# A recommender on one core: wide row buffers, scores summed in one PSUM bank, and an item stage with its products in PSUM

## The chip, the core and the metric

The kernel runs on one core of a Trainium2 chip. Its time is device microseconds from start to end of one launch. A core has five engines with their own instruction queues: TensorE (PE; its weight loads are listed apart as PEld), VectorE (DVE), ScalarE (ACT), GpSimd (POOL) and SyncE (SP). They meet through semaphores. SBUF is the working memory with 128 partitions; PSUM is the memory that TensorE writes, in banks of 512 float32 values per partition, eight of them. All data here is float32.

## The reference

Two stages follow each other. The first makes, for each of 50,001 items, two attention vectors over its 32 neighbours. The second scores 100 history positions of each of 16,384 users against the user's target item.

```python
def _neighbor_attn(E, near_full):                 # E_in or E_out, 50001 x 32
    V = E[near_full]                              # 50001 x 32 neighbours x 32
    scores = einsum('nd,nkd->nk', E, V) / sqrt(32)
    w = softmax(scores, axis=-1)
    return einsum('nk,nkd->nd', w, V)
a_sus = _neighbor_attn(E_in, near_full)
a_inf = _neighbor_attn(E_out, near_full)
h = concat([E_hist[history], a_sus[history], a_inf[history]])    # users x 100 x 128
t = concat([E_tgt[target], a_inf[target], a_sus[target]])        # users x 128
x = h * t[:, None, :]
z = relu(einsum('bld,hd->blh', x, W1) + b1)       # 128 hidden
scores = einsum('blh,h->bl', z, W2[0])
exp_A = exp(scores) * ((history != target[:, None]) & (history != 0))
denom = sum(exp_A, axis=-1) ** 0.5
s = sum(h * (exp_A / denom[:, None])[..., None])  # one number for all users
pred = dot(s, t) / (|s| * |t|)                    # s broadcast to 128 values
return sigmoid(pred)
```

Because only the sum over everything is needed of `h * attn`, a position enters `s` as its weight times the sum of its row's 128 values.

## The kernel before

**Item stage** (lines 106 to 257). Items are taken 128 at a time, one item to a partition: a *sub*, 391 of them, in 23 loads of 17 subs. For each sub POOL issues 32 indirect DMAs (`gather`, L136), one per neighbour; each fetches 128 rows of 64 values, that neighbour's E_in and E_out for each of the 128 items, into a buffer `v` (a ring of five subs). On DVE follow `products` (L152: `v` times the items' own rows, which ACT has copied into PSUM at L146; 2,048 values per partition, written to `prod` in SBUF), `scores` (L162: sums over 32), `largest` (L170, L171), on ACT `exponents` (L179, with the sums), then on DVE `weighted` (L192, once for each table: `v` times the exponents, written to `wv` in SBUF in the order d, k), `attend` (L203 a reciprocal, L205 sums over the neighbours) and `attended` (L212). `prod` and `wv` have one buffer each, in the pool `n_p`. In each turn of the loop POOL gets the gathers of sub s, DVE first the weighted rows of sub s-2, then the products and scores of sub s-1; a row is finished three subs late. After 17 subs the finished rows go to a table in DRAM: 129 values per item, first the sum of the other 128.

**User stage** (lines 268 to 408). Users are taken 128 at a time (a *chunk*, 128 of them) and positions 4 at a time (a *group*, 25 in a chunk), 3,200 groups in all. For each group s:

- `gather(s)`: POOL issues 4 indirect DMAs (L325), each fetching one position's row of 129 values for the 128 users, into a row buffer `h`. The ring has HBUF = 20 such buffers, one group each.
- `turn(s)`: PE turns the 4 row blocks by transposes into PSUM, `hT_ps` (L341, 3 banks).
- `times_target(s)`: DVE multiplies by the turned target row (L346, 128x512, PSUM to SBUF), and copies the 4 row sums of the group to `hsum` (L349, 128x4). That copy is the last reader of the row buffer. A declaration (L353, L354) tells the planner that the copy needs no wait of its own on the gathers, since PE has already read the rows.
- `hidden(s-3)`: PE multiplies W1 by the 512 columns into `z_ps` (L358, 3 banks), and ACT adds the bias and takes the relu (L360).
- `scored(s-6)`: PE makes the 4 positions' scores (L367): each of the four blocks of z, 128x128, is the stationary operand, and W2, one column, is the moving one, so that a score column of 128 users results. The chunk's 100 columns lie in one bank, `score`.

Every float32 product on PE shows as two passes, each with its own weight load, where it is a matmul, and as one where it is a transpose. Once per chunk POOL fetches the next chunk's target rows (`target_rows`, L289, at group 5), PE, DVE and ACT prepare them (`target_work`, L301 to L315, at group 15), and, after a chunk's last score, ACT takes the exponents of the 100 scores (`weights`, L373) and two groups later DVE masks, weighs with `hsum` and sums (`ended`, L378 to L381).

The order of the work is written out by hand for PE, ACT, DVE, SP and, in the user stage, POOL: each engine runs its instructions in the order of the calls in the loop at L388. POOL's queue holds only the gathers and the target rows there; it may run ahead of PE until the ring of row buffers is full. A short last stage (lines 410 to 440) makes `s` and the predictions.

Of the kernel before, what the change touches and what calls it, by code (L numbers as in the profile page):

```python
# [10 lines left out]
F32 = mybir.dt.float32  # L11
# [3 lines left out]
AF = mybir.ActivationFunctionType  # L15
# [3 lines left out]
P = 128  # L19
ITEMS = 50001  # L20
K = 32
G = 32
DE = 64
D = 128
HID = 128
B = 16384
L = 100
# [14 lines left out]
UC = B // P  # L42
BSUB = 4
LG = 4
NG = L // LG
W = 1 + D
LAG = 3
HBUF = 20

# [1 line left out]
def kernel(  # L53
# [52 lines left out]
    with (  # L106
        tc.manual_schedule(engines={E.Activation, E.DVE, E.SP}),
        tc.tile_pool(name="n_in", bufs=2) as n_in,
        tc.tile_pool(name="n_v", bufs=5) as n_v,
        tc.tile_pool(name="n_p", bufs=1) as n_p,  # L110
        tc.tile_pool(name="n_s", bufs=3) as n_s,
        tc.tile_pool(name="n_ps", bufs=2, space=bass.MemoryType.PSUM) as n_ps,
    ):
        its = {}
        subs = {}
# [32 lines left out]

        def products(s):
            v = subs[s]["v"]  # L150
            prod = n_p.tile([P, K, 2, G], F32, name="prod")
            nc.vector.tensor_tensor(  # L152
                prod.rearrange("p k t d -> p k (t d)"),
                v.rearrange("p k t d -> p k (t d)"),
                subs[s]["own"].to_broadcast([P, K, 2 * G]),
                ALU.mult,
            )
            subs[s]["prod"] = prod
# [29 lines left out]

        def weighted(s, t):
            if t == 0:  # L190
                subs[s]["wv"] = n_p.tile([P, 2, G, K], F32, name="wv")
            nc.vector.tensor_tensor(  # L192
                subs[s]["wv"][:, t].rearrange("p d k -> p k d"),
                subs[s]["v"][:, :, t, :],
                subs[s]["ex"][0][:, t, :]
                .rearrange("p (k o) -> p k o", o=1)
                .to_broadcast([P, K, G]),
                ALU.mult,
            )
# [67 lines left out]
    nc.vector.tensor_copy(tidf, tidx)  # L267
    with (
        tc.manual_schedule(engines={E.PE, E.Activation, E.DVE, E.SP, E.Pool}),
        tc.tile_pool(name="u_in", bufs=4) as u_in,  # L270
        tc.tile_pool(name="u_t", bufs=3) as u_t,
        tc.tile_pool(name="u_h", bufs=HBUF) as u_h,
        tc.tile_pool(name="u_x", bufs=6) as u_x,
        tc.tile_pool(name="u_z", bufs=6) as u_z,
        tc.tile_pool(name="u_s", bufs=3) as u_s,
        tc.tile_pool(name="ps_t", bufs=3, space=bass.MemoryType.PSUM) as ps_t,
        tc.tile_pool(name="ps_z", bufs=3, space=bass.MemoryType.PSUM) as ps_z,
        tc.tile_pool(name="ps_s", bufs=2, space=bass.MemoryType.PSUM) as ps_s,
    ):
        users, hists = {}, {}  # L280
        rows, got, hT, xT, z = {}, {}, {}, {}, {}

        def history_of(i):
            hists[i] = u_in.tile([P, BSUB, L], I32, name="hidx")
            nc.sync.dma_start(hists[i], hist_v[i])

        def target_rows(c):
            t = u_t.tile([P, D], F32, name="t")
            nc.gpsimd.indirect_dma_start(  # L289
                out=t,  # L290
                out_offset=None,
                in_=ttab[0:ITEMS, :],
                in_offset=bass.IndirectOffsetOnAxis(ap=tidx[:, c : c + 1], axis=0),
            )
            users[c] = {"t": t, "hidx": hists[c // BSUB][:, c % BSUB, :]}

        def target_work(c):
            u = users[c]
            t = u["t"]
            tT_ps = ps_t.tile([P, LG, P], F32, name="hT_ps")  # L300
            nc.tensor.transpose(tT_ps[:, 0, :], t, ident)  # L301
            tT = u_t.tile([D, 1, P], F32, name="tT")
            nc.vector.tensor_copy(tT[:, 0, :], tT_ps[:, 0, :])  # L303
            u["tT"] = tT
            nc.vector.tensor_reduce(tsum[:, c : c + 1], t, AX.X, ALU.add)
            junk = u_t.tile([P, D], F32, name="junk")
            nc.scalar.activation(junk, t, AF.Square, accum_out=tsq[:, c : c + 1])
            keep = u_s.tile([P, L], F32, name="keep")
            idf = u_s.tile([P, L], F32, name="idf")
            nc.vector.tensor_copy(idf, u["hidx"])  # L310
            nc.vector.tensor_scalar(keep, idf, 0.0, None, ALU.not_equal)  # L311
            nc.vector.scalar_tensor_tensor(
                keep, idf, tidf[:, c : c + 1], keep, ALU.not_equal, ALU.mult
            )
            u["keep"] = keep  # L315
            u["hsum"] = u_s.tile([P, L], F32, name="hsum")

        def gather(s):
            c, g = divmod(s, NG)
            rows[s] = u_h.tile([P, LG, W], F32, name="h")  # L320
            got[s] = []
            for q in range(LG):
                l = g * LG + q
                got[s].append(
                    nc.gpsimd.indirect_dma_start(  # L325
                        out=rows[s][:, q, :],
                        out_offset=None,
                        in_=table,
                        in_offset=bass.IndirectOffsetOnAxis(
                            ap=users[c]["hidx"][:, l : l + 1], axis=0  # L330
                        ),
                    )
                )

        def turn(s):
            c, g = divmod(s, NG)
            if g == 0:
                users[c]["score"] = ps_s.tile([P, L], F32, name="score")
            hT[s] = ps_t.tile([P, LG, P], F32, name="hT_ps")
            for q in range(LG):  # L340
                nc.tensor.transpose(hT[s][:, q, :], rows[s][:, q, 1:W], ident)  # L341

        def times_target(s):
            c, g = divmod(s, NG)
            xT[s] = u_x.tile([D, LG, P], F32, name="xT")
            nc.vector.tensor_tensor(  # L346
                xT[s], hT.pop(s), users[c]["tT"].to_broadcast([D, LG, P]), ALU.mult
            )
            copy = nc.vector.tensor_copy(  # L349
                users[c]["hsum"][:, g * LG : (g + 1) * LG],  # L350
                rows.pop(s)[:, :, 0:1].rearrange("p q o -> p (q o)"),
            )
            for one in got.pop(s):  # L353
                tc.declare_no_dep(copy.ins, one.ins, reason="TensorE has read the row")  # L354

        def hidden(s):
            z_ps = ps_z.tile([HID, LG, P], F32, name="z_ps")
            nc.tensor.matmul(z_ps, w1T, xT.pop(s), start=True, stop=True)  # L358
            z[s] = u_z.tile([HID, LG, P], F32, name="z")
            nc.scalar.activation(z[s], z_ps, AF.Relu, bias=b1_sb)  # L360

        def scored(s):
            c, g = divmod(s, NG)
            of = z.pop(s)
            for q in range(LG):
                l = g * LG + q
                nc.tensor.matmul(  # L367
                    users[c]["score"][:, l : l + 1], of[:, q, :], w2_sb, start=True, stop=True
                )

        def weights(c):
            users[c]["ea"] = u_s.tile([P, L], F32, name="ea")
            nc.scalar.activation(users[c]["ea"], users[c]["score"], AF.Exp)  # L373

        def ended(c):
            u = users.pop(c)
            ea = u["ea"]
            nc.vector.tensor_tensor(ea, ea, u["keep"], ALU.mult)  # L378
            nc.vector.tensor_reduce(den[:, c : c + 1], ea, AX.X, ALU.add)
            nc.vector.tensor_tensor(ea, ea, u["hsum"], ALU.mult)  # L380
            nc.vector.tensor_reduce(num[:, c : c + 1], ea, AX.X, ALU.add)  # L381

        last = UC * NG
        history_of(0)
        history_of(1)
        target_rows(0)
        target_work(0)
        for s in range(last + 2 * LAG + 4):  # L388
            c, g = divmod(s, NG)
            if s < last:  # L390
                if g == 0 and c % BSUB == 2 and 0 < c // BSUB and c // BSUB + 1 < UC // BSUB:
                    history_of(c // BSUB + 1)
                if g == 5 and c + 1 < UC:
                    target_rows(c + 1)
                gather(s)
                turn(s)
                times_target(s)
            if 0 <= s - LAG < last:
                hidden(s - LAG)
            if 0 <= s - 2 * LAG < last:  # L400
                scored(s - 2 * LAG)
            if s < last and g == 15 and c + 1 < UC:
                target_work(c + 1)
            done, left = divmod(s - 2 * LAG - NG, NG)
            if 0 <= done < UC and left == 0:
                weights(done)
            if 0 <= done < UC and left == 2:
                ended(done)

    with (  # L410
# [85 lines left out]
```

## Time and profile before

| | before |
| --- | --- |
| median of 3 runs | 36,684.49 us (36,681.49 to 36,691.43) |
| the profiled execution | 36,756.47 us, span 36,754.7 us |
| POOL, busy | 25,507.5 us, 69% |
| PE, PEld, busy | 10,981.4 us, 8,186.8 us |
| DVE, ACT, busy | 7,047.7 us, 2,610.8 us |
| item stage's gathers (L136) | 12,512, of 1,063 ns |
| user stage's gathers (L325) | 12,800, of 944 ns |
| mean granted clock of TensorE | 0.806 |

The profile is of one execution, which took 0.2% more than the median. Busy time is the time that an engine spends in its instructions. A gather on POOL is the issuing of the DMA, not the transfer, and the time between two instructions of an engine is its idle time, for which the profile names the event that ended it: `<-PE hT_ps L341` is a release by that PE instruction, `<-issue` means that nothing the profile shows was waited for, `<-remote` an event that it couldn't place. The granted clock is the share of full speed at which TensorE was let run: 1.00 in the item stage, where it does nothing, 0.63 on average in the user stage. In a timeline the columns are the start in us, the duration in us (the whole of a run of several equal instructions, x4 or so), the engine, the line, the operation, output and input, and in brackets the idle time ahead and what ended it.

### The profile page before, as it was taken

The numbers are of one execution on the slowest core, as the hardware profiler recorded it, in microseconds if no ns is written. First come the engines' busy times: TensorE is split into PE (matmuls) and PEld (weight loads), VectorE is DVE, ScalarE is ACT, GpSimd is POOL, SyncE is SP. The second block draws the span as 40 slices with busy tenths as digits, with TensorE's granted clock in tenths as the row PEclk, the third lists the DMA queues.
The fourth block names the chain that finished last, engine by engine and source line by source line (L and its number), as shares of the span: only waits on it lengthen the run. The fifth ranks groups of instructions, "written<-read, shape, count | busy, mean of one in ns | idle before, by whom it ended". The sixth has DMA issues, their size and how long they took to land. (4 is left out here: it accounts for less than half of the span.)

```text
span 36754.7 us, 143134 instructions
## 1 busy us (share of the span) xinstructions
PE 10981.4 (30%) x44931; PEld 8186.8 (22%) x44931; DVE 7047.7 (19%) x11109; ACT 2610.8 (7%) x5939; POOL 25507.5 (69%) x25446
## 2 busy tenths in 40 slices
PE   0000000000000000000455555555655555555555
PEld 0000000000000000000344444444444444444444
DVE  2222222222222222222111111111111111111111
ACT  0000000000000000000011111111111111111111
POOL 7777777777777777777666666666666666666665
PEclk9999999999999999999766666666666666666666
DMA  2111111111111111111222222222222222222221
GB/s 45 27 27 27 28 29 27 27 27 28 29 27 27 27 28 29 27 27 25 46 45 46 45 45 45 45 45 45 46 45 45 45 45 45 45 45 46 45 45 42
DMA packets 1028113, 1364.80 MB, mean 37 GB/s; under 512 B 559904, under 2 KB 614432, under 8 KB 1027360
## 3 DMA queue, kind: packets, MB, share of 16 engines
q0 software_dynamic: 814080, 1265.42, 16.4%
q10 hardware_dynamic: 151056, 51.51, 0.8%
q1 hardware_dynamic: 62224, 38.72, 0.4%
q8 instruction: 363, 5.95, 0.1%
q14 instruction: 390, 3.19, 0.0%
HBM read 1315.31 MB, written 51.50 MB: 37 GB/s over the span
## 5 line engine op out<-in xcount | busy, mean ns | idle before, releaser
L325 POOL DMA_INDIRECT h<-table,hidx x12800 | 12082.2, 944 | 6909.5 <-issue 3729.2
L136 POOL DMA_INDIRECT v<-in_egeo_dram,nidx x12512 | 13303.8, 1063 | 4199.3 <-issue 4100.5
L367 PEld LDWEIGHTS score<-w_sb,z 128*128 128x128 f32 x25600 | 5121.1, 264 | 7324.3 <-issue 7320.0
L367 PE MATMUL score<-w_sb,z 128*128 128x1 f32 x25600 | 4332.3, 273 | 5204.9 <-issue 5113.3
L301 PE MATMUL hT_ps<-ident,t 128*128 128x128 f32 x128 | 51.7, 404 | 17563.1 <-DMA t<-ttab,tidx 17527.7
L346 DVE TENSOR_TENSOR xT<-hT_ps,tT 128x512 f32<-128x512 f32 x3200 | 2190.4, 688 | 16114.5 <-PE hT_ps L341 7697.5
L358 PE MATMUL z_ps<-xT,w1T 128*128 128x512 f32 x6400 | 5005.9, 868 | 591.3 <-issue 588.1
L301 PEld LDWEIGHTS hT_ps<-ident,t 128*128 128x128 f32 x128 | 37.5, 293 | 17567.4 <-issue 17567.4
L341 PE MATMUL hT_ps<-ident,h 128*128 128x128 f32 x12800 | 3058.8, 360 | 2398.3 <-issue 1944.6
L360 ACT ACTIVATE z<-z_ps,b_sb 128x512 f32<-128x512 f32 x3200 | 2141.1, 687 | 17012.9 <-remote 6338.4
L152 DVE TENSOR_TENSOR prod<-v,own_ps 128x2048 f32<-128x2048 f32 x391 | 894.1, 2287 | 12667.3 <-DMA v<-in_egeo_dram,nidx 12667.1
L341 PEld LDWEIGHTS hT_ps<-ident,h 128*128 128x128 f32 x12800 | 2227.0, 205 | 2779.0 <-issue 2252.2
L358 PEld LDWEIGHTS z_ps<-xT,w1T 128*128 128x128 f32 x6400 | 1439.6, 270 | 881.5 <-issue 880.6
L192 DVE TENSOR_TENSOR wv<-v,ex 128x1024 f32<-128x1024 f32 x782 | 1407.6, 1876 | 341.9 <-ACT ex L179 240.0
L179 ACT ACTIVATE ex<-sc,top 128x32 f32<-128x32 f32 x782 | 227.7, 291 | 16996.0 <-DVE top L170 11999.4
L162 DVE TENSOR_REDUCE sc<-prod 128x64 f32<-128x2048 f32 x391 | 894.5, 2288 | 13.6
L205 DVE TENSOR_REDUCE att<-wv 128x64 f32<-128x2048 f32 x391 | 893.7, 2286 | 12.7
L349 DVE COPY hsum<-h 128x4 f32<-128x4 f32 x3200 | 544.0, 170 | 0.0
L289 POOL DMA_INDIRECT t<-ttab,tidx x128 | 120.8, 944 | 66.1 <-issue 65.2
L179 ACT ACTIVATION_READ_ACCUMULATOR ex<-sc,top 128x1 f32 x782 | 145.7, 186 | 0.0
L303 DVE COPY tT<-hT_ps 128x128 f32<-128x128 f32 x128 | 37.0, 289 | 423.8 <-remote 180.7
L212 DVE TENSOR_TENSOR row<-att,tot 128x64 f32<-128x64 f32 x391 | 88.1, 225 | 13.6
(50 smaller groups left out, 809.0 us busy)
## 6 DMA issues: line engine op xcount, KB each, us to landing
h<-table,hidx POOLq DMA_INDIRECT x12800
v<-in_egeo_dram,nidx POOLq DMA_INDIRECT x12512
table<-row ACTq DMA_DIRECT2D x22, 1096.5 KB
own<-in_egeo_dram SPq DMA_DIRECT2D x23, 544.0 KB
row<-in_ehist_dram SPq DMA_DIRECT2D x23, 544.0 KB
ttab<-in_etgt_dram ACTq DMA_DIRECT2D x1, 12500.0 KB
ttab<-row ACTq DMA_DIRECT2D x22, 544.0 KB
hidx<-in_history_dram SPq DMA_DIRECT2D x32, 200.0 KB
```

The lines of the kernel that those rows point to most:

```text
L136: nc.gpsimd.indirect_dma_start(out=v[:, k].rearrange("p t d -> p (t d)"), out_offset=None, in_=egeo, in_offset=bass.IndirectOffsetOnAxis(a ...
L152: nc.vector.tensor_tensor(prod.rearrange("p k t d -> p k (t d)"), v.rearrange("p k t d -> p k (t d)"), subs[s]["own"].to_broadcast([P, K, ...
L162: nc.vector.tensor_reduce(sc.rearrange("p t k -> p k t"), subs[s]["prod"], AX.X, ALU.add)
L192: nc.vector.tensor_tensor(subs[s]["wv"][:, t].rearrange("p d k -> p k d"), subs[s]["v"][:, :, t, :], subs[s]["ex"][0][:, t, :] .rearrange( ...
L205: nc.vector.tensor_reduce(att, subs[s]["wv"], AX.X, ALU.add)
L325: nc.gpsimd.indirect_dma_start(out=rows[s][:, q, :], out_offset=None, in_=table, in_offset=bass.IndirectOffsetOnAxis(ap=users[c]["hidx"][: ...
L341: nc.tensor.transpose(hT[s][:, q, :], rows[s][:, q, 1:W], ident)
L346: nc.vector.tensor_tensor(xT[s], hT.pop(s), users[c]["tT"].to_broadcast([D, LG, P]), ALU.mult)
L349: copy = nc.vector.tensor_copy(users[c]["hsum"][:, g * LG : (g + 1) * LG], rows.pop(s)[:, :, 0:1].rearrange("p q o -> p (q o)"),)
L358: nc.tensor.matmul(z_ps, w1T, xT.pop(s), start=True, stop=True)
L360: nc.scalar.activation(z[s], z_ps, AF.Relu, bias=b1_sb)
L367: nc.tensor.matmul(users[c]["score"][:, l : l + 1], of[:, q, :], w2_sb, start=True, stop=True)
```

## The change

- Row buffers. A buffer `h` now holds HG = 5 groups, 20 positions, and the ring has HBUF = 5 of them. Gathers write slices of it; PE and DVE read slices of it. The row sums are copied once for five groups (128x20), after the fifth of them has been multiplied; that copy is the last reader of the buffer. The declaration now names the 20 gathers.
- Scores. W2 is now the stationary operand: a group's weights are a window of 25 columns on a padded row `w2_row`, with W2 in column g and zeros elsewhere, and the group's z, 512 columns, is the moving operand. The 25 groups' products are accumulated in one PSUM bank, `turned` (25x512): row g gets group g's scores, the other rows get zeros added. When the chunk is done ACT copies the bank to SBUF (`kept`, one 25x512 copy), two groups later PE turns it back by four transposes (`turned_back`) into `score` (128 users x 4 x 25), and the exponents and the closing sums follow four and six groups after the last score, where they followed at zero and two. The loop runs four turns longer.
- PSUM. The hidden products have two banks instead of three; `score` has one bank of its own, `turned` two.
- Item stage. The pool `n_p` is gone: `prod` and `wv` share one PSUM tile, `big`, of four banks, with one buffer.

```diff
-HBUF = 20
+HG = 5
+HBUF = 5
...
-        tc.tile_pool(name="n_p", bufs=1) as n_p,
+        tc.tile_pool(name="n_pb", bufs=1, space=bass.MemoryType.PSUM) as n_pb,
...
-            prod = n_p.tile([P, K, 2, G], F32, name="prod")
+            prod = n_pb.tile([P, K * 2 * G], F32, name="big")
+            prod = prod.rearrange("p (k t d) -> p k t d", k=K, t=2)
...
-                subs[s]["wv"] = n_p.tile([P, 2, G, K], F32, name="wv")
+                wv = n_pb.tile([P, K * 2 * G], F32, name="big")
+                subs[s]["wv"] = wv.rearrange("p (t d k) -> p t d k", t=2, k=K)
...
-        tc.tile_pool(name="ps_z", bufs=3, space=bass.MemoryType.PSUM) as ps_z,
+        tc.tile_pool(name="ps_z", bufs=2, space=bass.MemoryType.PSUM) as ps_z,
...
+        tc.tile_pool(name="ps_1", bufs=1, space=bass.MemoryType.PSUM) as ps_1,
...
+        w2_row = u_1.tile([HID, 2 * NG - 1], F32, name="w2_row")
+        nc.vector.memset(w2_row, 0.0)
+        nc.vector.tensor_copy(w2_row[:, NG - 1 : NG], w2_sb)
...
-            rows[s] = u_h.tile([P, LG, W], F32, name="h")
-            got[s] = []
+            k = g % HG
+            if k == 0:
+                wide[s] = u_h.tile([P, HG * LG, W], F32, name="h")
+                got[s] = []
+            rows[s] = wide[s - k][:, k * LG : (k + 1) * LG, :]
...
+            rows.pop(s)
+            if g % HG < HG - 1:
+                return
+            s0, l = s - HG + 1, (g - HG + 1) * LG
             copy = nc.vector.tensor_copy(
-                users[c]["hsum"][:, g * LG : (g + 1) * LG],
-                rows.pop(s)[:, :, 0:1].rearrange("p q o -> p (q o)"),
-            )
-            for one in got.pop(s):
+                users[c]["hsum"][:, l : l + HG * LG],
+                wide.pop(s0)[:, :, 0:1].rearrange("p q o -> p (q o)"),
+            )
+            for one in got.pop(s0):
                 tc.declare_no_dep(copy.ins, one.ins, reason="TensorE has read the row")
...
+            if g == 0:
+                users[c]["turned"] = ps_s.tile([NG, LG * P], F32, name="turned")
+            nc.tensor.matmul(
+                users[c]["turned"],
+                w2_row[:, NG - 1 - g : 2 * NG - 1 - g],
+                of.rearrange("h q p -> h (q p)"),
+                start=g == 0,
+                stop=g == NG - 1,
+            )
+
+        def kept(c):
+            users[c]["by_g"] = u_s.tile([NG, LG * P], F32, name="by_g")
+            nc.scalar.copy(users[c]["by_g"], users[c]["turned"])
+
+        def turned_back(c):
+            users[c]["score"] = ps_1.tile([P, LG, NG], F32, name="score")
             for q in range(LG):
-                l = g * LG + q
-                nc.tensor.matmul(
-                    users[c]["score"][:, l : l + 1], of[:, q, :], w2_sb, start=True, stop=True
+                nc.tensor.transpose(
+                    users[c]["score"][:, q, :],
+                    users[c]["by_g"][:, q * P : (q + 1) * P],
+                    ident[0:NG, 0:NG],
                 )
...
-        for s in range(last + 2 * LAG + 4):
+        for s in range(last + 2 * LAG + 8):
...
             if 0 <= done < UC and left == 0:
+                kept(done)
+            if 0 <= done < UC and left == 2:
+                turned_back(done)
+            if 0 <= done < UC and left == 4:
                 weights(done)
-            if 0 <= done < UC and left == 2:
+            if 0 <= done < UC and left == 6:
                 ended(done)
```

More of the change, by code (lines that the diff above doesn't have):

```diff
@@ L269 @@
         tc.manual_schedule(engines={E.PE, E.Activation, E.DVE, E.SP, E.Pool}),
+        tc.tile_pool(name="u_1", bufs=1) as u_1,
         tc.tile_pool(name="u_in", bufs=4) as u_in,
@@ L276 @@
         tc.tile_pool(name="ps_t", bufs=3, space=bass.MemoryType.PSUM) as ps_t,
-        tc.tile_pool(name="ps_z", bufs=3, space=bass.MemoryType.PSUM) as ps_z,
+        tc.tile_pool(name="ps_z", bufs=2, space=bass.MemoryType.PSUM) as ps_z,
         tc.tile_pool(name="ps_s", bufs=2, space=bass.MemoryType.PSUM) as ps_s,
+        tc.tile_pool(name="ps_1", bufs=1, space=bass.MemoryType.PSUM) as ps_1,
     ):
+        w2_row = u_1.tile([HID, 2 * NG - 1], F32, name="w2_row")
+        nc.vector.memset(w2_row, 0.0)
+        nc.vector.tensor_copy(w2_row[:, NG - 1 : NG], w2_sb)
         users, hists = {}, {}
-        rows, got, hT, xT, z = {}, {}, {}, {}, {}
+        wide, rows, got, hT, xT, z = {}, {}, {}, {}, {}, {}
         def history_of(i):
@@ L319, in gather @@
             c, g = divmod(s, NG)
-            rows[s] = u_h.tile([P, LG, W], F32, name="h")
-            got[s] = []
+            k = g % HG
[3 more added lines that the diff above has]
+            rows[s] = wide[s - k][:, k * LG : (k + 1) * LG, :]
             for q in range(LG):
                 l = g * LG + q
-                got[s].append(
+                got[s - k].append(
                     nc.gpsimd.indirect_dma_start(
@@ L336, in turn @@
             c, g = divmod(s, NG)
-            if g == 0:
-                users[c]["score"] = ps_s.tile([P, L], F32, name="score")
             hT[s] = ps_t.tile([P, LG, P], F32, name="hT_ps")
@@ L372, in weights @@
             users[c]["ea"] = u_s.tile([P, L], F32, name="ea")
-            nc.scalar.activation(users[c]["ea"], users[c]["score"], AF.Exp)
+            nc.scalar.activation(
+                users[c]["ea"].rearrange("p (g q) -> p q g", q=LG), users[c]["score"], AF.Exp
+            )
         def ended(c):
```

## The prediction

> **What bounds the kernel now.** The page's first part comes first: the fullest engine is POOL, which issues the gathers, and it is busy for only 69%. Then the costliest groups (busy us, mean ns of one, then the idle time ahead of them).
>
> ```profile
> L325 POOL DMA_INDIRECT h<-table,hidx x12800 | 12082.2, 944 | 6909.5 <-issue 3729.2
> L136 POOL DMA_INDIRECT v<-in_egeo_dram,nidx x12512 | 13303.8, 1063 | 4199.3 <-issue 4100.5
> L367 PEld LDWEIGHTS score<-w_sb,z 128*128 128x128 f32 x25600 | 5121.1, 264 | 7324.3 <-issue 7320.0
> ```
>
> Busy and idle of the two gather groups add to 17,503 us (item stage) and 18,992 us (user stage; 19,179 with the 128 target gathers, 120.8 + 66.1). That is the whole span of 36,754.7 but for 73 us, so POOL's pace is the time, and each of its idles counts. Next, busy time by stretch, one stretch inside each stage (PE, PEld, DVE, ACT, POOL, then granted clock, DMA share, GB/s).
>
> ```profile
> 300.00:17500.00 17200.00, 0.00 (x0) 0.00 (x0) 4301.94 (x3473) 402.94 (x2298) 13079.33 (x12278) 1.00 0.14 27
> 17600.00:36650.00 19050.00, 10872.99 (x44469) 8111.80 (x44469) 2624.96 (x7473) 2168.57 (x3547) 12131.33 (x12852) 0.63 0.20 45
> ```
>
> The DMA engines are 14 to 20% busy, DVE 25 and 14%, ACT 2 and 11%: none is a bound. A gather costs 17,200 / 12,278 = 1.401 us in the first stage and 19,050 / 12,852 = 1.482 us in the second. Then the timeline, a late piece of the item stage first.
>
> ```profile
> 8024.29 0.94 POOL L136 DMA_INDIRECT v<-in_egeo_dram,nidx  x1 [0.30 <-issue]
> ...
> 8043.80 1.79 POOL L136 DMA_INDIRECT v<-in_egeo_dram,nidx  x1 [0.30 <-issue]
> ...
> 8047.25 2.29 DVE L152 TENSOR_TENSOR prod<-v,own_ps 128x2048 f32<-128x2048 f32 x1 [32.65 <-DMA v<-in_egeo_dram,nidx]
> 8047.85 1.24 POOL L136 DMA_INDIRECT v<-in_egeo_dram,nidx  x1 [0.86 <-issue]
> ```
>
> An undisturbed gather comes every 0.944 + 0.30 = 1.2475 us. Some are stretched, here two of them before DVE's block begins. Products come 40.0 us apart (32 x 1.2475) for the first 285 us and 44.80 us apart (32 x 1.400) ever after, with the same DVE work in both: POOL has a second pace of 1.400 us that the trace doesn't name. In the user stage:
>
> ```profile
> 18080.29 0.94 POOL L325 DMA_INDIRECT h<-table,hidx  x1 [5.17 <-remote]
> ...
> 18108.99 0.94 POOL L325 DMA_INDIRECT h<-table,hidx  x1 [0.30 <-issue]
> 18114.45 0.94 POOL L325 DMA_INDIRECT h<-table,hidx  x1 [4.51 <-remote]
> ```
>
> ```profile
> 18086.47 0.63 PE L341 MATMUL hT_ps<-ident,h 128*128 128x128 f32 x4
> 18086.94 1.02 PE L358 MATMUL z_ps<-xT,w1T 128*128 128x512 f32 x2
> 18087.80 0.95 PE L367 MATMUL score<-w_sb,z 128*128 128x1 f32 x8
> 18088.61 0.63 PE L341 MATMUL hT_ps<-ident,h 128*128 128x128 f32 x4
> ...
> 18101.67 0.37 PE L341 MATMUL hT_ps<-ident,h 128*128 128x128 f32 x1 [1.73 <-issue]
> 18103.10 0.37 PE L341 MATMUL hT_ps<-ident,h 128*128 128x128 f32 x1 [1.06 <-issue]
> 18105.92 0.37 PE L341 MATMUL hT_ps<-ident,h 128*128 128x128 f32 x1 [2.45 <-issue]
> ```
>
> POOL issues 24 gathers at 1.2475, then stops because all 20 row buffers are taken. PE does a group in 2.14 us (18086.47 to 18088.61), far faster than POOL feeds it, and then falls to about one instruction per us while waiting for nothing that the profile shows. Over the stage's 580 or so such cycles: POOL runs for 29.7 us (median, 24.25 gathers, 6 groups); PE executes about 148 rows (142 to 156; loads, matmuls and a semaphore row per group) at pace and crawls at about 1.05 rows per us; some us after POOL has stopped PE is fast again, at half clock first, and frees a buffer. A line through the stalls, stall against the run before it, is 0.10 x run + 2.6 us. So the stall has a part in proportion to the gathers and a fixed part, and PE pays by the instruction.
>
> **The change part by part.** The sum is made against the profiled execution's own 36,756.5; the median of the runs is 36,684.5, 72 us (0.2%) below, and I take those off at the end.
>
> *Scores.* Now a group is 4 transposes, 1 hidden product, 4 score products, each in two rows per pass: 8 + 4 + 16 = 28 rows and a semaphore. L367 loses its four loads of z; one product of 512 columns has the shape of L358, 4 rows. After: 16 + 1, and 8 rows of the turned-back transposes per 25 groups (0.3): 17.3 or so. The 148 rows then last 148 / 17.4 = 8.5 groups instead of 5.1. At pace these take some 24 us (half clock first); the crawl of the other 26 us of a 50 us run adds 27 rows, 1.6 groups. So one cycle holds about 10 groups. POOL's run is 40.4 gathers x 1.2475 = 50.4 us, the stall by the line 7.6, together 58.0 us, 5.80 per group; worked the other way, 40.4 x 1.400 + 1.65 of idle (what the cycle of 35.6 us now has over 24.25 x 1.400) is 58.2. The same line gives now (30.25 + 5.6) / 6 = 5.97, and the stage's own figure is 19,179 / 3,200 = 5.99. The gain is 0.17 us per group, 3,200 x 0.17 = -545. PE's rows themselves are on no path: bounds are 0 (the stall goes by gathers alone) and -3,050 (rival 2).
>
> *Row buffers.* The ring holds 25 groups for 20, but a buffer is freed only when its fifth group has been turned, so POOL stops only at multiples of 5 groups. A cycle of 10 fits that; but where PE is k groups short when the crawl ends, POOL waits for them, at 4.16 us each at half clock (L341 at 25032.56 and again at 25036.72). PE's capacity by the rows (8.5 + 1.6 = 10.1 groups) is so near to 10 that I take a mean k of 0.1 per cycle: 0.1 x 4.16 / 10 x 3,200 = +130. Bounds: 0 (k = 0), and k = 3 in cycles of 15 groups, (75.6 + 10.2 + 12.5) / 15 = 6.55, +1,800. Fewer copies: L349 has 3,200 x 170 ns = 544 us of DVE, after it 640 longer ones. DVE waits for PE here (14% busy), so 0; with that cover gone, 3,200 x 0.17 = -544 at the most. The gathers beside the copies last 944 ns like all others.
>
> The Trainium skill (SBUF — State Buffer, "Who interferes with whom") says that an fp32 copy from SBUF to SBUF on DVE shuts GpSimd out of a shared port, so that gathers' descriptors can't be written; by it merging the copies would give up to 544 us. The row is against it, and the sum has 0.
>
> *ACT's copy, turning back.* 128 copies of 25x512 by L360's 687 ns: 88 us on ACT (11% busy); queued behind it is only the next group's relu, and PE, which is three groups from needing that. 0; uncovered, 88. The four transposes: 128 x 0.89 us (four at half clock, 25032.56 to 25033.45) = 114 us of PE, beside POOL's run: 0. PE waits for the copy two groups after it was released, 4.3 us at full pace for 0.69 us: 0; were the wait to fall in each chunk's crawl, one median stall, 128 x 5.95 = 760. A product of L358's kind takes 1.71 us at half clock where four of L367 take 1.57, so a group needs 4.30 for 4.16 there: within the k above. Two hidden banks for three: the relu's 0.69 us lies within two groups' 4.3 us: 0; were PE to wait for each, a group would take 2.18 + 0.69 at pace, still under POOL's 5.04. Memset and copy of the padded weights, ending four groups later: +3 at the ends.
>
> *Products in PSUM.* Per sub-tile DVE has 2.29 + 2.29 + 0.4 + 3.60 + 0.15 + 2.29 + 0.22 = 11.2 us in 44.8, with 32.65 idle. One shared buffer brings no wait: products follow the weighted rows and their sum on the same engine now. If PSUM doubled or halved its ops it would change 11 us under 33 us of slack: 0. Where POOL's 1.400 is DVE's doing, up to 12,278 x (1.401 - 1.2475) = 1,885 could come back; since gathers beside L192 at 136 us took 0.94 and one beside nothing at 8043.80 took 1.79, I take 0. I see no reason for a loss.
>
> The same section says that DVE locks that port only in modes which need both of its ports; and that one input from SBUF beside one from PSUM doesn't contend. That is what L152 and L192 have already, so by the rule the move brings nothing, 0 as well; by the trace's worst reading it could bring 1,885. No run here shows the lock.
>
> *Sum.* 36,756.5 - 545 + 130 + 3 + 0 = 36,345 in a profiled execution; less 72: 36,270.
>
> **The rivals.**
> 1. *The ring by fives makes POOL wait (slower).* For it: POOL stops only at boundaries, and PE crawls exactly then. With PE one group short in each cycle of 10 it adds 0.416 a group, 1,330, to the gain of 545: +785, 37,470; with k = 1.6, 38,270; with cycles of 15, +1,800. It decides from k = 0.17 / 0.416 = 0.4 groups per cycle. Against it: PE has 50 us for 10 groups and needs 24 for 8.5 of them.
> 2. *PE's rows released wholly.* If PE needs fewer rows than it is ever short of, POOL never stops: 12,928 x 1.2475 = 16,128, that is -3,050: 33,630. Against it: 174 rows in 50 us are still more than 148, and the item stage shows 1.400 with no PE at all.
> 3. *The item stage freed by PSUM outputs.* Half of 1,885 beside the user stage's -410: 35,330.
> 4. *Nothing measurable* (±0.2%, ±73 us, about what a measurement here can tell from no change): the stall is in proportion to gathers after all, or k near 0.4 eats the gain: 36,680.
>
> **How the numbers follow.** Forecast 0.41 (own range 35,950 to 36,600), slower ring 0.30, nothing 0.09, item stage 0.12, rows released 0.08. Faster: 0.41 + 0.12 + 0.08 = 0.61, less 0.03 for the forecast's own edge = 0.58; same 0.09 + 0.01 = 0.10; slower 0.30 + 0.02 = 0.32. Range: 35,100 leaves out the released rows (0.08); 37,700 leaves out the ring at its worst (0.12).
>
> **What would show it.** PE rows of L367 6,400 instead of 25,600, its loads the same. POOL's runs 40 gathers long (step right) or 20 or 60 with stalls of 10 us and more (ring). Item products still 44.80 us apart; 40 would be rival 3. Idle ahead of L325 down from 6,910 to some 6,500. Wrong if PE's crawl isn't counted in rows, or if POOL's stalls sit at wide boundaries with PE at half clock.

## The result

The changed kernel takes 37,143.5 us (37,102.1 to 37,151.5, four runs) where the kernel before, beside it, took 36,683.0 (36,681.4 to 36,691.4): 1.0123 times as long, 95% interval 1.0105 to 1.0140. It was forecast at 36,270, and is 460 us slower. The profiled execution of the changed kernel took 37,138.2 us, 5 under its median, with a span of 37,136.4.

The costliest groups of the page after (busy us, mean ns of one, then the idle time ahead):

```profile
L336 POOL DMA_INDIRECT h<-table,hidx x12800 | 12106.1, 946 | 7264.2 <-issue 5017.8
L137 POOL DMA_INDIRECT v<-in_egeo_dram,nidx x12512 | 13334.4, 1066 | 4162.2 <-issue 4072.2
...
L380 PE MATMUL turned<-z,w_row 128*25 128x512 f32 x6400 | 4051.6, 721 | 0.0
```

Busy and idle of the item stage's gathers add to 17,497 us, where they were 17,503: nothing happened there. In the user stage they are 19,370 for 18,992, +378 of the 382 us between the two profiled executions; 355 of it is idle time. PE executes 26,243 matmuls for 44,931, so the scores did shrink as the diff says. What PE does with its time is in the waits (us in total, times, longest). Before, the list had no wait of PE for the relu among its leading entries; after, it has this one:

```profile
PE z_ps L371 <- ACT z L373: 7623.2, 812, 18.9
...
POOL h L336 <- PE z_ps L371: 2031.9, 175, 15.9
```

PE waits 812 times for ACT's relu to free one of the two hidden banks, and POOL waits for PE behind it. But the relu takes 0.69 us. The timeline shows why PE waits 10 us and more for it:

```profile
25088.58 0.66 PE L350 MATMUL hT_ps<-ident,h 128*128 128x128 f32 x4
...
25089.07 1.02 PE L371 MATMUL z_ps<-xT,w1T 128*128 128x512 f32 x2
...
25092.54 1.12 PE L371 MATMUL z_ps<-xT,w1T 128*128 128x512 f32 x2 [0.89 <-ACT z L373]
...
25102.38 0.69 DVE L355 TENSOR_TENSOR xT<-hT_ps,tT 128x512 f32<-128x512 f32 x1 [11.91 <-issue]
25107.28 0.69 ACT L373 ACTIVATE z<-z_ps,b_sb 128x512 f32<-128x512 f32 x1 [14.79 <-issue]
...
25108.02 2.08 PE L371 MATMUL z_ps<-xT,w1T 128*128 128x512 f32 x2 [12.80 <-ACT z L373]
```

DVE's product at 25102.38 uses the transposes that ended at 25089.2; ACT's relu at 25107.28 reads the hidden product that ended at 25090.1. They start 13 and 17 us after what they read was done, and the engines were idle for the 11.91 and 14.79 us just before. The trace's semaphore events say that the signal is late, not its reader: PE's last instruction here ends at 25095.22 and its next starts at 25108.02, but its semaphore is still counted up at 25095.33, 25096.76, 25098.85 and 25100.26. Such delays are called late signals below. From transposes to product a quarter of all groups have a delay of at most 0.04 us, half one of 2 us or more, a quarter one of 21 us or more. The kernel before has such delays too (upper quartile 18 us); the prediction took the slow PE beside them for the whole of the matter.

A stop of POOL in the changed kernel, from its last gather before to its first after it:

```profile
25061.97 0.94 POOL L336 DMA_INDIRECT h<-table,hidx  x1 [0.30 <-issue]
...
25069.55 1.29 DVE L355 TENSOR_TENSOR xT<-hT_ps,tT 128x512 f32<-128x512 f32 x2 [11.95 <-remote]
...
25071.81 0.68 DVE L355 TENSOR_TENSOR xT<-hT_ps,tT 128x512 f32<-128x512 f32 x1
...
25074.65 0.69 DVE L355 TENSOR_TENSOR xT<-hT_ps,tT 128x512 f32<-128x512 f32 x1 [2.16 <-PE hT_ps L350]
25075.26 0.17 DVE L362 COPY hsum<-h 128x20 f32<-128x20 f32 x1
...
25076.17 0.94 POOL L336 DMA_INDIRECT h<-table,hidx  x1 [13.26 <-PE z_ps L371]
```

POOL stops at 25062.9. 6.6 us later the first late signal is in and DVE multiplies the buffer's second group; the third, fourth and fifth have to pass too before the copy frees the buffer, which takes another 6.6 us. In the kernel before, one group would have been enough. All stops of each profile (idles of POOL over 1 us in the user stage) were counted in this way; *first* is the time from POOL's last instruction to DVE's first product, *rest* from there to the next gather, *share* is stop over run.

| kernel | stops | mean run, us | mean stop | first | rest | share |
| --- | --- | --- | --- | --- | --- | --- |
| before | 580 | 27.5 | 5.49 | 4.14 | 1.35 | 0.200 |
| changed | 336 | 47.7 | 10.31 | 5.29 | 5.02 | 0.216 |

### The profile page after: what moved, and what is told of

The parts are those of the page before. It is cut to its first block, busy times and chain, and to the rows that moved or that the text cites. A ratio compares the mean times of both kernels' runs of the same rounds, so it can differ in the third digit from the quotient of the medians.

```text
span 37136.4 us, 101163 instructions
## 1 busy us (share of the span) xinstructions
PE 9953.4 (27%) x26243; PEld 3129.5 (8%) x26243; DVE 6464.7 (17%) x8551; ACT 2715.3 (7%) x6067; POOL 25562.3 (69%) x25446
## 4 chain that ended last, share of the span: by engine, by line
POOL 35%; another core or an unknown queue 32%; PE 16%; issue 14%; ACT 2%; DVE 0%; DMA 0%; POOLq 0%; DVEq 0%; SPq 0%; ACTq 0%
POOL v L137 35%; PE z_ps L371 6%; PE turned L380 6%; PE hT_ps L350 3%; ACT z L373 2%; POOL h L336 0%; PE score L395 0%; PE hT_ps L309 0%; DVE xT L355 0%; DVE big L195 0%; DVE big L154 0%; DVE sc L164 0%; DVE att L208 0%; ACT junk L315 0%
## 5 line engine op out<-in xcount | busy, mean ns | idle before, releaser
L371 PE MATMUL z_ps<-xT,w1T 128*128 128x512 f32 x6400 | 4262.7, 754 | 9009.4 <-ACT z L373 7623.2
L380 PE MATMUL turned<-z,w_row 128*25 128x512 f32 x6400 | 4051.6, 721 | 0.0
L154 DVE TENSOR_TENSOR big<-v,own_ps 128x2048 f32<-128x2048 f32 x391 | 897.7, 2296 | 13083.4 <-DMA v<-in_egeo_dram,nidx 13083.1
L350 PE MATMUL hT_ps<-ident,h 128*128 128x128 f32 x12800 | 2367.6, 313 | 634.4 <-DVE xT L355 318.2
L371 PEld LDWEIGHTS z_ps<-xT,w1T 128*128 128x128 f32 x6400 | 1177.1, 230 | 9299.9 <-ACT z L373 7871.4
L350 PEld LDWEIGHTS hT_ps<-ident,h 128*128 128x128 f32 x12800 | 1531.9, 155 | 3789.9 <-issue 3137.8
L195 DVE TENSOR_TENSOR big<-v,ex 128x1024 f32<-128x1024 f32 x782 | 960.8, 1229 | 356.1 <-ACT ex L181 199.6
L164 DVE TENSOR_REDUCE sc<-big 128x64 f32<-128x2048 f32 x391 | 896.4, 2292 | 13.4
L208 DVE TENSOR_REDUCE att<-big 128x64 f32<-128x2048 f32 x391 | 895.8, 2291 | 0.0
L380 PEld LDWEIGHTS turned<-z,w_row 128*25 128x25 f32 x6400 | 433.3, 109 | 3112.6 <-issue 3112.6
```

Of the source, the lines that this page charges most:

```text
L154: nc.vector.tensor_tensor(prod.rearrange("p k t d -> p k (t d)"), v.rearrange("p k t d -> p k (t d)"), subs[s]["own"].to_broadcast([P, K, ...
L164: nc.vector.tensor_reduce(sc.rearrange("p t k -> p k t"), subs[s]["prod"], AX.X, ALU.add)
L195: nc.vector.tensor_tensor(subs[s]["wv"][:, t].rearrange("p d k -> p k d"), subs[s]["v"][:, :, t, :], subs[s]["ex"][0][:, t, :] .rearrange( ...
L208: nc.vector.tensor_reduce(att, subs[s]["wv"], AX.X, ALU.add)
L380: nc.tensor.matmul(users[c]["turned"], w2_row[:, NG - 1 - g : 2 * NG - 1 - g], of.rearrange("h q p -> h (q p)"), start=g == 0, stop=g == N ...
```

## The experiments

The experiments ran on four chips, so each ratio is against the kernel before on the same chip. The chips are of two kinds. On two of them the kernel before takes 36,530 to 36,551 us, close to the 36,683 of the first runs (whose chip isn't on record); on the other two 31,844. Chips of the first kind are called chip A here, those of the second chip B. Between runs on the two chips A, differences of some 20 us mean nothing.

**Theory A:** the freeing by fives makes POOL wait for the rest of a five. **Theory B:** the longer cycle itself does, whatever the freeing.

### The changed kernel with 25 buffers of one group

```diff
-HG = 5
-HBUF = 5
+HG = 1
+HBUF = 25
```

> The changed kernel with HG = 1 and HBUF = 25: the same space for 25 groups and all other parts, but each group's buffer freed by itself. Theory A (the buffers freed by fives make POOL wait for the rest of a five): after a stop POOL waits for PE to come round (about 5 us) and then for 1.5 us as before, not 5.4; some 9 groups per cycle, 5.8 us a group, time 36,050 to 36,300, faster than before. Theory B (PE's signals come late in the longer runs, two hidden banks instead of three, whatever the freeing): 37,000 to 37,200, as the changed kernel.

Measured on chip A: 36,224.6 us, 0.9912 of before (0.9895 to 0.9928). Faster than before, with all other parts of the change in. The rest falls to 1.18 us. The runs don't grow to the 9 groups expected: they are 6 long on average, 7 in the median.

### The kernel before with buffers of five groups alone

```diff
-HBUF = 20
+HG = 5
+HBUF = 5
...
-            rows[s] = u_h.tile([P, LG, W], F32, name="h")
+            if k == 0:
+                wide[s] = u_h.tile([P, HG * LG, W], F32, name="h")
+            rows[s] = wide[s - k][:, k * LG : (k + 1) * LG, :]
```

> The kernel before with only the row buffers of five groups (HG = 5, HBUF = 5); scores and item stage as before. Theory A: slower than before, since POOL stops only at multiples of five and PE with its 28 rows a group is one to two groups short: +300 to +1,500, that is 37,000 to 38,200. Theory B: the buffers alone change nothing, 36,680 within 75.

Measured on chip A: 37,481.8, 1.0255 (1.0238 to 1.0272), +931 us. Rest 4.34 us. The two runs agree with theory A and not with B: the buffers of five groups make the kernel slower even with three hidden banks and four score products, as before.

### The item stage alone

```diff
-            prod = n_p.tile([P, K, 2, G], F32, name="prod")
+            prod = n_pb.tile([P, K * 2 * G], F32, name="big")
```

> The kernel before with only the item stage's products and weighted rows in PSUM. Both theories: 36,680 within 75, and products 44.80 us apart from 0.3 ms on.

Measured on chip A: 1.0001 (0.9991 to 1.0010), products 44.80 us apart. DVE's weighted rows did get faster (960.4 us in this run); the kernel before and the changed kernel in the groups by line:

```profile
L192 DVE TENSOR_TENSOR wv<-v,ex 128x1024 f32<-128x1024 f32 x782 | 1407.6, 1876 | 341.9 <-ACT ex L179 240.0 <-issue 101.9
```

```profile
L195 DVE TENSOR_TENSOR big<-v,ex 128x1024 f32<-128x1024 f32 x782 | 960.8, 1229 | 356.1 <-ACT ex L181 199.6 <-issue 143.0
```

The 447 us that DVE saves go to idle time, since it waits for gathers.

### The scores alone, with 20 buffers of one group and two hidden banks

```diff
-                nc.tensor.matmul(
-                    users[c]["score"][:, l : l + 1], of[:, q, :], w2_sb, start=True, stop=True
+            nc.tensor.matmul(
+                users[c]["turned"],
+                w2_row[:, NG - 1 - g : 2 * NG - 1 - g],
+                of.rearrange("h q p -> h (q p)"),
```

> The kernel before with only the scores summed in one bank (with two hidden banks), ring of 20 single groups. Theory A: the gain that the prediction gave to the scores, -400 to -600: 36,100 to 36,300. Theory B: at or above before, 36,700 to 37,200.

Measured on chip A: 36,209.2, 0.9906 (0.9890 to 0.9923), -341 us: theory A's side, at less than its size (-400 to -600 was expected). 25 buffers for 20 add nothing (0.9912, with the item stage's change in).

### Three hidden banks, and six buffers of five

The changed kernel's new wait, PE for ACT's relu, asks whether the two banks matter by themselves.

```diff
-        tc.tile_pool(name="ps_z", bufs=2, space=bass.MemoryType.PSUM) as ps_z,
-        tc.tile_pool(name="ps_s", bufs=2, space=bass.MemoryType.PSUM) as ps_s,
+        tc.tile_pool(name="ps_z", bufs=3, space=bass.MemoryType.PSUM) as ps_z,
+        tc.tile_pool(name="ps_s", bufs=1, space=bass.MemoryType.PSUM) as ps_s,
```

> The changed kernel with three hidden banks as before (its summing bank has one buffer instead of two). Its trace shows a new wait, PE 7,623 us for ACT's relu to free one of the two hidden banks. Theory A (rest of the five): PE's wait is only where its late signals show; time as the changed kernel, 1.012 of before, within 0.003. Rival: two hidden banks are what holds PE back, and the time falls by 300 us or more, to 1.003 or less.

This run came on chip B: 31,840.9, 0.9999 (0.9989 to 1.0009), and so did the next three: the changed kernel (31,842.2), three banks (31,840.8) and six buffers (31,840.6), each 0.9999 of before. What was expected of them:

> The changed kernel itself on the chip of these runs. Where before takes 36,550: 1.010 to 1.016, that is the buffers by fives cost 700 to 800 us against the same space by single groups (0.991). Where before takes 31,840: 1.000.

> The changed kernel with three hidden banks (one summing bank), beside the changed kernel on the same chip, which the first run of it lacked. Where before takes 36,550: if the two banks hold PE back (7,623 us of PE's waits end with ACT's relu), 300 us or more faster than the changed kernel; if that wait is only where late signals show, within 100 us of it.

> The changed kernel with six buffers of five groups (30 groups of space). If it is the freeing by fives that costs: POOL's runs are longer or equal and the wait after DVE's first product stays near 5 us; time within 150 us of the changed kernel. If it is space that POOL lacks: 500 us faster or more.

There POOL never stops, as the waits of the changed kernel there show: no wait of POOL in the user stage is longer than the 0.30 us between two gathers.

```profile
POOL h L336 <- issue: 3814.1, 12515, 0.3
```

The same three then ran on chip A:

> The changed kernel again, on the other chip if it comes: where before takes 36,550, 1.010 to 1.016.

> Three hidden banks, one summing bank. Where before takes 36,550: if the two banks hold PE back, 300 us or more faster than the changed kernel; if PE's wait for ACT is only where late signals show, within 100 us of it.

> Six buffers of five groups. Where before takes 36,550: if the freeing by fives costs, within 150 us of the changed kernel; if POOL lacks space, 500 us faster or more.

```diff
-HBUF = 5
+HBUF = 6
```

Measured: the changed kernel 36,865.5, 1.0088 (1.0071 to 1.0105), a little under the 1.010 expected; three hidden banks 36,429.0, 0.9975 (0.9964 to 0.9986); six buffers 36,889.7, 1.0098 (1.0082 to 1.0115). Space is not what POOL lacks. But the third bank is worth 437 us in this kernel, and with it the changed kernel is 0.25% faster than before (a small but clear difference): here the expectation of theory A, within 100 us, fell. The 437 are net of what the smaller ring of summing banks costs; PE's waits for ACT's copy of that bank are 448 us in total. The waits of PE that answer to the line in the result, with two banks and with three:

```profile
PE z_ps L371 <- ACT z L373: 7835.9, 811, 18.8
...
PE hT_ps L350 <- DVE xT L355: 215.8, 48, 8.4
```

```profile
PE hT_ps L350 <- DVE xT L355: 3701.1, 537, 15.6
...
PE z_ps L371 <- ACT z L373: 1780.3, 579, 5.7
```

With three banks PE waits less for the relu and more for DVE to free a transpose bank. The rest is shorter, 3.47 us for 5.17, at equal runs; that PE is one group further when the late signals come in would explain it, but wasn't counted.

### Pauses on POOL

**Theory C:** the late signals come of gathers issued faster, at 1.2475 us, than something takes them, at about 1.40, the pace that POOL falls to in the item stage. **Theory D:** PE is held back beside gathers at any pace. A pause on POOL, after each group's four gathers, tells them apart; to the kernel's bound engine it only adds work.

```diff
+        rest = u_p.tile([P, 512], F32, name="rest")
...
+        def pause():
+            nc.gpsimd.memset(rest, 0.0)
...
                 gather(s)
+                pause()
                 turn(s)
```

> Scores in one bank with 20 single buffers (the faster kernel of the first experiments) and, after each group's four gathers in the user stage, a memset of 128x512 on POOL, which by the 206 ns of a 128x128 one takes some 0.5 us: gathers at 1.38 us on average. Theory C (PE's signals are late because gathers are issued faster than the 1.400 us at which something takes them; below that pace they aren't late): no stops of POOL, 3,200 x 5.6 = 17,900 in the user stage, 600 to 800 less than without the pause, 0.97 of before. Theory D (PE is held back beside gathers at any pace): the pauses come on top, 3,200 x 0.5 = +1,600, 1.03 of before.

> The same with a memset of 128x256, some 0.3 us, gathers at 1.32 us on average. Theory C: half of the excess pace is left, longer runs and shorter stops, 0.975 to 0.985 of before. Theory D: +900, 1.015.

> The kernel before, scores by four products a group, with the pause of 128x512. Theory C: PE is never late, so that its rows don't matter: 0.97 of before, as with scores in one bank. Theory D: +1,600, 1.04.

All three came on chip B: 1.0409, 1.0193 and 1.0409 of before. No stops were there to save, so the pauses are paid in full: 3,200 of them add 1,303 us with 512 columns (33,147.3 - 31,844.4, in the kernel before), 0.41 us each of the memset's 543 ns. The next four were written for either chip and came on chip A.

> Scores in one bank, 20 single buffers, the pause of 128x512 (543 ns, which added 0.406 us per group net where POOL never stopped): 1.349 us per gather on average. Two sorts of chip are told apart by the kernel before beside it: about 31,840 (no late signals, POOL never stops) or about 36,600. On the first: 1.041 of before again. On the second, theory C (late signals come of gathers issued faster than about 1.38 us): few stops, user stage near 3,200 x 5.45 = 17,440 against 18,610 without the pause, 0.96 to 0.975 of before. Theory D (late beside gathers at any pace): 1.02 to 1.03.

> The same with 128x768 (0.75 us, some 0.61 net): 1.40 us per gather. Where before takes 31,840: +1,950, 1.061. Where it takes 36,600: theory C has no stops at all and a user stage of 3,200 x 5.65 = 18,080, 0.975 to 0.985; theory D 1.04.

> The changed kernel, buffers freed by fives, with the pause of 128x512. Where before takes 31,840: 1.041. Where it takes 36,600: by theories A and C together, PE in time means that a five is free in time, and the time is that of the single buffers with the same pause within 100 us; by D 1.035 to 1.05.

> The kernel before, for its profile on this chip. Where it takes 31,840, DVE follows the transposes within 0.1 us all the way and item products are 39.95 us apart; where it takes 36,600, as in the trace of before.

Measured: scores in one bank with the pause of 512 columns 36,092.1, 0.9878 (0.9862 to 0.9895); with 768 columns 35,897.2, 0.9825 (0.9809 to 0.9842); the changed kernel, by fives, with 512 columns 36,333.9, 0.9950 (0.9933 to 0.9967). The kernel before took 36,549.2 in its own profile there (one run), with signals as late as in the first one (upper quartile 18 us). With 768 columns a group's gathers come every 5.63 us, 1.41 us a gather:

```profile
25007.36 0.75 POOL L348 MEMSET rest<- 128x768 f32 x1
25008.28 0.97 POOL L337 DMA_INDIRECT h<-table,hidx  x1 [0.17 <-issue]
...
25012.99 0.76 POOL L348 MEMSET rest<- 128x768 f32 x1
25013.91 0.95 POOL L337 DMA_INDIRECT h<-table,hidx  x1 [0.17 <-issue]
```

and POOL's idle time is near that of chip B (3,666 us, pauses apart, for 3,472 in the same kernel with 512 columns there):

```profile
L337 POOL DMA_INDIRECT h<-table,hidx x12800 | 12101.4, 945 | 3666.2 <-issue 3465.4
```

Giving POOL 2,420 us more to do made the kernel 312 us faster than without it. Theory D's times (1.02 to 1.05 of before) are out. Theory C is right on the stops with 768 columns, not on the signals: at 1.41 us a gather the stops are nearly gone (61, 148 us in all), but half of DVE's products still start 11 us or more after their transposes, for 5 us without the pause. That signals are late beside gathers at any pace, as theory D has it, isn't refuted on chip A. The delay seems to cost nothing while POOL's lead of 20 groups covers it. With 512 columns 276 stops remain, and the time, 0.9878, lies outside theory C's 0.96 to 0.975. By theories A and C the fives were expected to come within 100 us of the single buffers at equal pause; they are 242 off, so the rest of the five still costs there.

All kernels on chip A but the item stage alone, in one table, counted as above (pauses are not counted as idle):

| kernel | time over before | stops | mean run | mean stop | first | rest | share |
| --- | --- | --- | --- | --- | --- | --- | --- |
| before | 1 | 571 | 28.0 | 5.18 | 3.89 | 1.29 | 0.185 |
| fives alone | 1.0255 | 455 | 35.1 | 8.54 | 4.19 | 4.34 | 0.243 |
| changed | 1.0088 | 326 | 49.1 | 10.04 | 4.86 | 5.17 | 0.204 |
| changed, six buffers | 1.0098 | 327 | 49.0 | 9.80 | 4.99 | 4.81 | 0.200 |
| changed, three hidden banks | 0.9975 | 326 | 49.0 | 8.51 | 5.04 | 3.47 | 0.173 |
| scores, 25 single | 0.9912 | 533 | 29.9 | 4.91 | 3.73 | 1.18 | 0.164 |
| scores, 20 single | 0.9906 | 503 | 31.7 | 5.21 | 3.92 | 1.29 | 0.164 |
| changed, pause 512 | 0.9950 | 216 | 80.2 | 6.02 | 3.59 | 2.43 | 0.075 |
| scores, 20 single, pause 512 | 0.9878 | 276 | 62.8 | 4.04 | 3.21 | 0.83 | 0.064 |
| scores, 20 single, pause 768 | 0.9825 | 61 | 295.3 | 2.42 | 1.64 | 0.78 | 0.008 |

In the kernels without a pause the order of the shares is the order of the times, but for the changed one and that with six buffers, which measure nearly the same. The last kernel is the quickest on chip A. It isn't one to keep without a thought: on chip B the pause of 512 columns, the smaller of the two, costs 4%. The scores with single buffers need no such choice. They weren't run on chip B, where the changed kernel, with the same scores, takes what the kernel before takes.

## Why the prediction was wrong

- **What bounds the kernel: right.** POOL's pace and its idles are the time, on both chips. The item stage brought nothing, as written; the copies of sums and ACT's copy weren't tried apart, but gathers last 944 to 946 ns beside 3,200 copies or 640. Where the trace allowed 1,885 us of DVE's doing in the item stage, the Trainium skill (SBUF — State Buffer, "Who interferes with whom") was the better guide: a DVE instruction with at most one SBUF input, outside the modes that use two ports, doesn't contend with GpSimd. With both outputs in PSUM the stage took 17,497 us for 17,503.
- **The line through the stalls: right as far as it goes.** By 0.10 x run + 2.6, single buffers with scores in one bank should stop 5.8 us after 31.7; they stop 5.2.
- **Scores, -545: the right sign, mis-sized.** Alone they bring -341. The step from rows to cycles failed: the 148 rows were to last for cycles of 10 groups, but with single buffers a run has 25 gathers on average (31.7 us), 6.3 groups, and 32 gathers, 8 groups, in the median. That the stage's level was met all the same (5.80 us a group predicted, 18,613 / 3,200 = 5.82 measured) is in part luck; it is the kernel before that takes less on chip A, 18,962 / 3,200 = 5.93 for 5.99. That PE pays by the row is at most a part of it: beside the gathers the signals of its work come late, and PE then waits for banks that are long read.
- **Row buffers, +130: the first step that failed.** Cycles came at 10 groups, as predicted (runs of 40 and 41 gathers are the commonest), but the k of 0.1, the groups that POOL still waits for in a cycle, was too small. The stop was put at 7.64 + 0.42 = 8.06 us; it is 10.31. The line gives 0.10 x 47.7 + 2.6 = 7.37 for such a run, and (10.31 - 7.37) / 4.16 makes k 0.7, above the 0.4 from which the prediction itself gave the case to rival 1. In time, freeing by fives costs 36,865 - 36,225 = 640 us in the changed kernel, and 931 alone.
- **"Two hidden banks for three: 0": the second.** The relu's 0.69 us does lie within two groups' time; what must be covered is the time until the relu has started and PE learns of its end, and it started 17 us late in the lines above. The third bank is worth 36,865 - 36,429 = 437 us in the changed kernel, whose stop with it is 8.51 us. With 437 in this step's place alone the forecast would have been no change, -415 + 437, not a gain.
- **The two overlap and can't be added.** With three banks fives cost 36,429 - 36,209 = 220 us against the scores with single buffers, but those have two banks, so that this isn't the price of the fives alone. And -341, +220 and +437 give the measured +336 within 20 us by necessity, since each is counted from the kernel of the one before it; the sum doesn't test how the loss is split.
- **The rivals.** Rival 1 named the side and the place, and with a k of 0.7 for its 1 its sum gives 0.7 x 1,330 - 545 = +386 for the measured +460 (0.30 for it was too little). Its reason, a PE one group short at half clock, is at most a part of it, as a third bank takes the loss away. Rivals 2 and 3 didn't occur on chip A. On chip B the changed kernel's POOL stops nowhere and its user stage takes 16,138 us, rival 2's 16,128, but the kernel before takes the same time there, so that it isn't the change's doing and the change is worth nothing.

Open: two hidden banks with single buffers cost an unknown part of the scores' gain, as single buffers with three banks weren't run. What takes the gathers at 1.40 us, and why PE's signals come late beside them, no run shows. One rival wasn't tried: the traces of chip A hold only a part of the semaphore events (PE's are 15,034 for 19,330 instructions that make one, in the changed kernel), those of chip B all of them (19,331). Whether the recording itself has a share in the late signals isn't known: no run on record was made to tell.

## What to carry to other kernels

Before a ring's buffers are merged, ask how many more pieces of work must pass before the next one comes free at the moment the issuing engine stops: equal space freed in larger pieces cost 640 us here (36,865 against 36,225, with two hidden banks), although it issued the same DMAs. Cost a PSUM bank that is taken away by the time until its reader starts and its writer goes on in the profile, not by the reader's duration. Two parts of a change that lengthen the same wait are costed together, not one by one. And where the fullest engine runs ahead and then stops, compare its pace while running with its pace over the whole: where something behind it can't keep that pace, slowing it may even gain, as on chip A; where it can, as on chip B, the pause is paid in full.

## What the runs showed of the hardware

- Chips of two kinds ran the same program in times 15% apart: 31,844 and 36,530 to 36,551 us for the kernel before. On chip B item products are 39.95 us apart throughout (median) and DVE follows PE's transposes within 0.24 us at all times in the changed kernel; on chip A the products are 44.80 apart from 0.3 ms on, and signals are up to 57 us late. The DMA engines' busy share in the user stage doesn't tell the kinds apart: it is 0.20 to 0.22 on chip A and 0.24 on B, in step with the time.
- The late signals have a grid. In the changed kernel on chip A 64% of the steps of 0.5 to 8 us between events of PE's semaphore in the user stage lie within 0.04 us of a multiple of 0.70 us (11% would by chance), on chip B 5%. The item stage's pace, 1.400 us, is two such steps; that both have one cause isn't shown.
- On chip A gathers are issued 1.2475 us apart but aren't kept at that. The item stage settles at 1.400 us; in the user stage a pause that brings them to 1.41 ends nearly all stops.
- A group with the summing product (25 columns of weights) takes longer on PE than estimated: in the changed kernel 2.42 us at a granted clock of 1.00 (25019.74 to 25022.16) and 4.75 at 0.50 (25010.00 to 25014.75), for 2.18 and 4.30. While POOL runs nothing waits for it; in the rest of a five it should count, which no run shows apart.
